# A fused conditional block on one core: the first sum of the ff activations as a ScalarE copy and an accumulating DMA

## The chip, the cores and the metric

The kernel runs on one core of a Trainium2 chip. The metric is the time of one execution on the device, in microseconds (us). The engines are TensorE (PE in the profile; its weight loads are PEld), VectorE (DVE), ScalarE (ACT), GpSimd (POOL) and SyncE (SP). Each works through its own queue in order; semaphores hold an instruction until what it needs is there, and everything behind it on that engine waits too.

## The reference

Two sequences of 2048 tokens with 512 features each pass one block. The modulation comes from a conditioning vector; then follow two residual branches, each with a normalization, two matrix products and a GELU:

```python
emb = jnp.dot(jax.nn.silu(t), ada_w) + ada_b
shift_msa, scale_msa, gate_msa, shift_mlp, scale_mlp, gate_mlp = jnp.split(emb, 6, axis=-1)
norm = _ln(x) * (1.0 + scale_msa[:, None]) + shift_msa[:, None]
h = jax.nn.gelu(jnp.dot(norm, ssm_w1) + ssm_b1, approximate=False)
x = x + gate_msa[:, None] * (jnp.dot(h, ssm_w2) + ssm_b2)
norm2 = _ln(x) * (1.0 + scale_mlp[:, None]) + shift_mlp[:, None]
hf = jax.nn.gelu(jnp.dot(norm2, ff_w1) + ff_b1, approximate=True)     # 512 -> 1024
x = x + gate_mlp[:, None] * (jnp.dot(hf, ff_w2) + ff_b2)              # 1024 -> 512
```

All is float32.

## The kernel before, in words

**Blocks and stages.** The 4096 tokens are cut into eight blocks of 512. Each block has four products: `hA` (x times `ssm_w1`), `oA` (its result times `ssm_w2`, added to x), `hC` (times `ff_w1`) and `oC` (times `ff_w2`, added to x). The gates are multiplied into the second weights beforehand. The stages of neighbouring blocks are interleaved: in step i of the loop over blocks (it starts at 1) come the products `hC` of block i, `oA` of block i+1, `oC` of block i, and `hA` of block i+2.

**Products of quarters.** Instead of eight products of quarter matrices a stage makes seven (named P1 to P7), whose operands are sums and differences of quarters. Where a quarter's product is cut once more in the same way, its seven smaller products are called leaves. For the activations of `hC` (the tile `hClo`, `hChi`: features on partitions, tokens in columns) the operands of the first level are made by `sums_of_first` (L388), once for each of two groups of features:

```python
lambda: cut_sum(eng, s[0], q["21"], q["22"], ALU.add, cut),        # P5
lambda: cut_sum(eng, s[1], s[0], q["11"], ALU.subtract, cut),      # P6
lambda: cut_sum(eng, q["21"], q["11"], q["21"], ALU.subtract, cut),# P7, in place
lambda: cut_sum(eng, s[2], q["12"], s[1], ALU.subtract, cut),      # P3
```

Each is one addition or subtraction of 128 partitions by 512 columns (L386). `q["21"]` is the second half of the group's columns in `hClo`, two runs of 256 floats on each partition; `q["22"]` the same in `hChi`; the three sums `s` lie in a tile `hSC` of their own. `first_operands` (L406) names them: P5 is `s[0]`, P4 is `q["22"]`, P7 is `q["21"]`.

**The order of the work.** Nothing is reordered by a scheduler: the program's order is the order in each engine's queue. Work for the other engines is hung into TensorE's stream by `hook(hooks, places, ops)` (L583): after the matmuls of a place (a number in the products of `hC`, a step name such as P1 or R4 in `oA`, a mark such as 0a in `oC`) the ops listed there are issued. `residual_with_leaves` (L906) runs the steps of `oA` in the order P1, R0, P5, R1, R2, P6, R3, R4, P7, R5, R6, and maps a hook's name to its step by `STEP_OF` (P2 to step P5, P5 to R4, P3 to R5, P4 to R6).

**Around the change.** In blocks 2, 3 and 5 (`SEVEN`, L1602) the last product `oC` is made wholly of leaves (`residual_in_all_leaves`, L1117). Its left operands need three layers of sums, all made on POOL:
- the four first-level sums of group 0, hung at place 20 of the `hC` products (L1685), and those of group 1, hung into `oA` (L1690);
- `sums24`, `sums356` and `sums17`: the leaves' sums of P2 and P4, of P5, P6 and P3, and of P1 and P7. Their first two steps go into `oA` (L1696, L1697) and, for `sums17` (written to a tile `leaves`, in block 5 to a free weight tile), to place 0a of `oC` (L1764). There, ahead of `sums17`, POOL also makes the power that gives the reciprocal root of the next normalization (`r`, L656), from a variance `ve` that DVE makes (L655) when the last row of `oA` is done.

Beside this ScalarE applies the GELU to the activations (L1278), normalizes a later block (L719), fills the accumulators with the bias (L529) and, after the first leaves of `oA`, copies an accumulator (`pl_oA_x` from `pl_oA_y`, L950) that TensorE goes on adding to. SP moves the transposed pieces of a later block (L739, `x<-blocks`, sixteen DMAs of 64 KB) at the same time. POOL begins no DMA.

Of the kernel before, what the change touches and what calls it, by code (L numbers as in the profile page):

```python
# [38 lines left out]
ALU = mybir.AluOpType  # L39
# [101 lines left out]
def kernel(  # L141
# [16 lines left out]
    nc = tc.nc  # L158
# [229 lines left out]
    def sums_of_first(q, s, eng, cut=1):  # L388

        return [  # L390
            lambda: cut_sum(eng, s[0], q["21"], q["22"], ALU.add, cut),
            lambda: cut_sum(eng, s[1], s[0], q["11"], ALU.subtract, cut),
            lambda: cut_sum(eng, q["21"], q["11"], q["21"], ALU.subtract, cut),
            lambda: cut_sum(eng, s[2], q["12"], s[1], ALU.subtract, cut),
        ]
# [146 lines left out]
    def apart_leaves(row, eng):  # L542
        v = row.rearrange("p (q e d) -> p q e d", q=2, e=2)
        eng.tensor_tensor(leaf_row, v[:, :, 1], v[:, :, 0], ALU.subtract)
# [38 lines left out]
    def hook(hooks, places, ops):  # L583

        for n, op in enumerate(ops):
            hooks.setdefault(places[min(n, len(places) - 1)], []).append(op)
# [623 lines left out]
    class First:  # L1210
# [29 lines left out]
        def __call__(self, p, j, k):  # L1240
            return self.ops[p][:, k, j * P : (j + 1) * P]

    class Second:
# [66 lines left out]
        def summed(self, g, eng, cut=1):  # L1310
# [4 lines left out]
            self.parts[g] = first_operands(q, s)  # L1315
            return sums_of_first(q, s, eng, cut)

        def __call__(self, p, j, k):
            return self.parts[k // 2][p][:, k % 2, j * P : (j + 1) * P]

# [138 lines left out]
    hooks = {}  # L1459
# [21 lines left out]
    hooks = {}  # L1481
# [28 lines left out]
    hooks = {}  # L1510
# [18 lines left out]
    hooks = {}  # L1529
# [12 lines left out]
    hC = Second(0)  # L1542
    n2[1] = Norm(1, 2)
    hooks = {}
# [25 lines left out]
    hooks = {}  # L1570
# [10 lines left out]
    hooks = {}  # L1581
# [7 lines left out]
    hooks = {}  # L1589
# [28 lines left out]
    for i in range(1, NBLK):  # L1618
        five, seven = True, i in SEVEN
        nxt, nx2, last = i + 1 < NBLK, i + 2 < NBLK, i + 1 == NBLK  # L1620
        ahead, alone = i + 3 == NBLK, not nx2
        hC = Second(i)
        hooks = {}
# [58 lines left out]
            hook(hooks, (4,), [lambda: apart_leaves(gb[5], nc.gpsimd)])  # L1682
        if i == 1:
            hook(hooks, (4,), [lambda: apart_leaves(gb[5], nc.gpsimd)])
        hook(hooks, (20,), hC.summed(0, nc.gpsimd))  # L1685
        hC.products(fa, fb[i], hooks, last or i == 1)

        hooks = {}
        hC_sums = hC.summed(1, nc.vector if alone else nc.gpsimd)
        hook(hooks, EARLY, hC_sums)  # L1690
        engs = (nc.vector if alone else nc.gpsimd, nc.gpsimd, nc.gpsimd)
        if seven:
# [12 lines left out]
        if nx2:  # L1705
# [26 lines left out]
            if ahead:  # L1732
                hooks = {}
# [10 lines left out]
        hooks = {}  # L1744
# [107 lines left out]
        hooks = {}  # L1852
# [81 lines left out]
```

## Time and profile before

| | before |
|---|---|
| median of 3 runs | 577.88 us (577.78 to 578.2) |
| the profiled execution | 577.74 us, its span 575.9 us |
| mean granted TensorE clock | 1.000 |
| DMA moved in the span | 62.30 MB, 108 GB/s on average |
| DMA queues | SP's and ScalarE's |

The profile is that of one execution, its span being the time from the first to the last instruction; the measured time of the same execution holds 1.8 us more. A row of the timeline gives the start, the duration, the engine, the line of the kernel, the operation, the tile written and the tiles read, the shape and the count; in square brackets the idle time ahead of it and what ended that. Rows that follow one another without a gap are merged and counted (x16). A row of groups gives the count, the busy time in us and the mean in ns, and then the idle time ahead and its releasers. Tile names are shortened: `hSC` is a tile of first-level sums, `forms` a buffer that holds the leaves' sums, `fw` and `w` are weights. An engine with `q` behind its name (SPq, ACTq) is the issuing of a DMA, not its transfer.

### The profile page before, as it was taken

The numbers are of one execution on the slowest core, as the hardware profiler recorded it, in microseconds if no ns is written. First come the engines' busy times: TensorE is split into PE (matmuls) and PEld (weight loads), VectorE is DVE, ScalarE is ACT, GpSimd is POOL, SyncE is SP. The second block draws the span as 40 slices with busy tenths as digits, with TensorE's granted clock in tenths as the row PEclk, the third lists the DMA queues.
The fourth block names the chain that finished last, engine by engine and source line by source line (L and its number), as shares of the span: only waits on it lengthen the run. The fifth ranks groups of instructions, "written<-read, shape, count | busy, mean of one in ns | idle before, by whom it ended". The sixth has DMA issues, their size and how long they took to land.

```text
span 575.9 us, 10119 instructions
## 1 busy us (share of the span) xinstructions
PE 570.8 (99%) x3443; PEld 514.1 (89%) x3443; DVE 453.6 (79%) x963; ACT 292.7 (51%) x574; POOL 436.7 (76%) x460
## 2 busy tenths in 40 slices
PE   8999999999999999999999999999999999999997
PEld 4888888888899889998899988998889999899897
DVE  4968898996878586987869877996768598897676
ACT  3727457705652875448734588326655431742430
POOL 1665449999949869889898999998994885379361
PEclk9999999999999999999999999999999999999999
DMA  8977333303205223283032930243240240031002
GB/s 329 390 232 249 100 71 92 96 38 146 58 18 162 106 100 69 97 260 126 1 93 50 330 115 21 54 109 122 101 109 2 110 126 23 1 73 74 2 1 73
DMA packets 26863, 62.30 MB, mean 108 GB/s; under 512 B 5136, under 2 KB 6204, under 8 KB 25148
## 3 DMA queue, kind: packets, MB, share of 16 engines
q1 hardware_dynamic: 22784, 55.87, 29.9%
q10 hardware_dynamic: 4028, 5.79, 3.9%
q8 instruction: 27, 0.44, 0.4%
q14 instruction: 24, 0.20, 0.1%
HBM read 35.94 MB, written 9.97 MB: 80 GB/s over the span
## 4 chain that ended last, share of the span: by engine, by line
PE 97%; DMA 2%; SPq 0%; DVE 0%; issue 0%; DVEq 0%
PE px_hC L1283 11%; PE py_hA L565 10%; PE py_hC L1283 8%; PE pv_hC L1283 8%; PE pl_oC_P_y L1038 5%; PE py_oC L990 5%; PE pv_hA L565 5%; PE py_oA L925 5%; PE pl_oC_A_y L1133 4%; PE py_oA L565 4%; PE pl_oC_P_v L1038 3%; PE pl_oC_B_y L1133 3%; PE py_hC L565 2%; PE px_hA L565 2%; PE py_oC L565 2%; PE pl_oA_y L940 2%
## 5 line engine op out<-in xcount | busy, mean ns | idle before, releaser
L656 POOL TENSOR_TENSOR r<-ve,minus_half 128x4 f32<-128x4 f32 x16 | 16.6, 1037 | 57.7 <-DVE ve L655 50.7
L767 ACT ACTIVATE nT<-nT,mod,mod 128x512 f32<-128x512 f32 x32 | 23.4, 803 | 46.2 <-DMA nT<-blocks 16.3
L1206 POOL TENSOR_TENSOR forms<-forms 128x256 f32<-128x256 f32 x56 | 42.5, 759 | 3.8 <-DVE forms L1202 0.4
L1283 PE MATMUL py_hC<-forms,fw 128*128 128x256 f32 x168 | 40.9, 379 | 0.0
L1300 DVE TENSOR_TENSOR hClo<-hClo,py_hC 128x512 f32<-128x512 f32 x42 | 28.5, 683 | 11.6 <-ACT hClo L1297 8.2
L719 ACT ACTIVATE nT<-x,nmr,rstd 128x512 f32<-128x512 f32 x36 | 26.8, 803 | 19.4 <-DVE nmr L704 16.8
L1283 PEld LDWEIGHTS py_hC<-forms,fw 128*128 128x128 f32 x168 | 31.7, 190 | 4.6 <-DVE hClo L1300 0.2
L386 POOL TENSOR_TENSOR hSC<-hClo,hChi 128x512 f32<-128x512 f32 (+1 forms) x16 | 19.2, 1205 | 18.7 <-ACT hChi L1278 17.9
L602 DVE BATCH_NORM_STATS2 st<-x 128x6 f32<-128x512 f32 x42 | 28.4, 675 | 4.9 <-DMA x<-in_x_dram 4.9
L1300 DVE TENSOR_TENSOR hChi<-hChi,pv_hC 128x512 f32<-128x512 f32 x35 | 23.2, 678 | 9.2 <-PE pv_hC L1283 5.0
L1278 ACT ACTIVATE hClo<-hClo,colsT 128x256 f32<-128x256 f32 x56 | 25.3, 498 | 5.0 <-DVE hClo L1300 4.8
L1283 PE MATMUL px_hC<-forms,fw 128*128 128x256 f32 x112 | 27.6, 379 | 0.0
L767 ACT ACTIVATE x<-x,mod 128x512 f32<-128x512 f32 x24 | 17.5, 801 | 18.8 <-DMA x<-blocks 18.8
L386 POOL TENSOR_TENSOR hClo<-hClo 128x512 f32<-128x512 f32 (+1 forms) x23 | 26.5, 1154 | 0.0
L1278 ACT ACTIVATE hChi<-hChi,colsT 128x256 f32<-128x256 f32 x56 | 25.1, 496 | 1.9 <-DVE hChi L1300 1.9
L730 DVE STREAM_TRANSPOSE blocks<-nT 128x512 f32<-128x512 f32 x36 | 24.2, 695 | 1.7 <-ACT nT L719 1.7
L1297 ACT ACTIVATE hChi<-py_hC 128x512 f32<-128x512 f32 x14 | 7.6, 594 | 34.0 <-PE py_hC L1283 14.8
L1297 ACT ACTIVATE hClo<-px_hC 128x512 f32<-128x512 f32 x21 | 12.5, 596 | 22.5 <-PE px_hC L1283 18.9
L1283 PEld LDWEIGHTS px_hC<-forms,fw 128*128 128x128 f32 x112 | 21.3, 190 | 2.9
L565 PE MATMUL py_hA<-x,w 128*128 128x256 f32 x96 | 22.7, 379 | 0.0
L1300 DVE TENSOR_TENSOR hChi<-hChi,px_hC 128x512 f32<-128x512 f32 x28 | 19.1, 682 | 4.3 <-ACT hClo L1297 2.1
L1283 PE MATMUL px_hC<-forms,fw_s 128*128 128x256 f32 x84 | 20.5, 380 | 0.0
(537 smaller groups left out, 1921.9 us busy)
## 6 DMA issues: line engine op xcount, KB each, us to landing
x<-in_x_dram SPq DMA_DIRECT2D x13, 1024.0 KB
out_dram<-x SPq DMA_DIRECT2D x14, 512.0 KB
x<-blocks SPq DMA_DIRECT2D x96, 64.0 KB
nT<-blocks SPq DMA_DIRECT2D x88, 64.0 KB
ada<-in_L_cond_ada_w_dram SPq DMA_DIRECT2D x5, 1024.0 KB
fw<-in_L_cond_ff_w_dram SPq DMA_DIRECT2D x2, 2048.0 KB
nT<-blocks ACTq DMA_DIRECT2D x56, 64.0 KB
w<-in_L_cond_ssm_w_dram SPq DMA_DIRECT2D x2, 1024.0 KB
```

Source lines behind the costliest of these rows:

```text
L386: eng.tensor_tensor(out[:, r], a[:, r], b[:, r], f)
L565: nc.tensor.matmul(ps[b][j * apart][:, j, :], lhs(p, j, k), rhs(p, j, k), start=(fresh and j * (not apart) == 0 and k == 0), stop=(p in (" ...
L602: nc.vector.bn_stats(st, xs[self.i][:, c, :])
L767: nc.scalar.activation(dst, src, AF.Identity, bias=shift, scale=scale)
L925: nc.tensor.matmul(ps[BANK[p]][:, j, :], hops(p, j, k), wops[p][:, k, :], start=False, stop=(k == KD // 2 - 1), skip_group_check=True,)
L990: yield lambda j=j, k=k: nc.tensor.matmul(ps[BANK[p]][:, j, :], hops(p, j, k), wops[p][:, k, :], start=False, stop=(k == kdim - 1), skip_g ...
L1038: nc.tensor.matmul(t[:, n, :], hops.leaves[p][f][:, k, :], leaf_wops[p][f][:, k, :], start=room not in started, stop=(f in ("P2", "P3", "P ...
L1133: nc.tensor.matmul(rooms[g, b][:, at[p], :], hops.leaves[p][f][:, k, :], leaf_wops[p][f][:, k, :], start=(g, b) not in started, stop=(f in ...
L1206: eng.tensor_tensor(reg[d], reg[a], reg[b], ALU.add if f == "+" else ALU.subtract)
L1278: nc.scalar.activation(h, h, AF.Gelu_apprx_tanh, bias=fb1T[:, m : m + 1])
L1283: nc.tensor.matmul(ps[b][:, j, :], fa[ra][:, j * P : (j + 1) * P], fb[rb].rearrange("p a (c q) -> p c a q", q=Q), start=(fresh and j == 0) ...
L1300: nc.vector.tensor_tensor(dest(d), dest(d), ps[b], op)
```

## The change

In blocks 2, 3 and 5 the first sum of each group (P5 = P7 + P4) is no longer an addition on POOL. ScalarE copies one operand into the sum's place, and then a DMA that POOL begins adds the other operand to it. The other three sums of each group stay on POOL, but the order changes: the third sum, which overwrites P7 and needs only the copy to be done, comes directly after the DMA's issue; the second and fourth sums of both groups, which need the DMA's result, go to later hooks of `oA`.

```diff
+        def added_by_dma(self, g):
+
+            p = self.parts[g]
+
+            def op():
+                nc.scalar.copy(p["P5"], p["P7"])
+                nc.gpsimd.dma_start(out=p["P5"], in_=p["P4"], accum_op=ALU.add)
+
+            return op
...
-        hook(hooks, (20,), hC.summed(0, nc.gpsimd))
+        sums_0 = hC.summed(0, nc.gpsimd)
+        if seven:
+            sums_1 = hC.summed(1, nc.gpsimd)
+            adds = [hC.added_by_dma(g) for g in range(2)]
+            hook(hooks, (20,), [adds[0], sums_0[2]])
+        else:
+            hook(hooks, (20,), sums_0)
         hC.products(fa, fb[i], hooks, last or i == 1)
 
         hooks = {}
-        hC_sums = hC.summed(1, nc.vector if alone else nc.gpsimd)
+        if seven:
+            hC_sums = [adds[1], sums_1[2], sums_0[1], sums_0[3], sums_1[1], sums_1[3]]
+        else:
+            hC_sums = hC.summed(1, nc.vector if alone else nc.gpsimd)
         hook(hooks, EARLY, hC_sums)
```

`EARLY` is P1, P2, P6, P5, P7, so the six ops of `hC_sums` go to the steps P1, P5, P6, R4, P7 and P7 of `oA`. On ScalarE the copy of group 0 comes behind the first bias copy into `py_oA` (L529), the copy of group 1 behind the last GELU of the block and ahead of the copy of `pl_oA_x` (L950). One such DMA takes 128 rows of two runs of 1 KB, 256 KB.

## The prediction

> **What bounds the kernel now.** I read the page's first lines and its chain that ended last, then the waits of TensorE, then busy time by stretches around blocks 2, 3 and 5.
>
> ```profile
> PE 570.8 (99%) x3443; PEld 514.1 (89%) x3443; DVE 453.6 (79%) x963; ACT 292.7 (51%) x574; POOL 436.7 (76%) x460
> ...
> PE 97%; DMA 2%; SPq 0%; DVE 0%; issue 0%; DVEq 0%
> ```
> ```profile
> engine line waited for: us in total, times, longest us
> PE idle L1392 <- POOL w_t masks.py:199: 1.3, 1, 1.3
> PE pada L304 <- DMA ada<-in_L_cond_ada_w_dram: 0.3, 1, 0.3
> ```
> ```profile
> core 0: us, PE busy (x) PEld busy (x) DVE busy (x) ACT busy (x) POOL busy (x), PEclk, DMA share, GB/s
> ...
> 215.00:262.00 47.00, 47.00 (x335) 44.55 (x334) 37.95 (x101) 24.68 (x48) 41.92 (x40) 1.00 0.46 135
> 283.00:330.00 47.00, 47.00 (x335) 44.55 (x334) 38.93 (x101) 23.55 (x45) 43.12 (x41) 1.00 0.45 138
> 422.00:480.00 58.00, 58.00 (x400) 54.64 (x399) 42.74 (x110) 24.41 (x46) 44.37 (x44) 1.00 0.29 90
> ```
>
> TensorE makes 97% of the chain. Its whole list of waits is 1.6 us, both before the first block. In the three stretches that the edit touches it is busy for 47.00 of 47.00, 47.00 of 47.00 and 58.00 of 58.00 us at a granted clock of 1.00. The edit leaves TensorE's stream as it is. So it can win nothing there; all it can do is make TensorE wait. The question is which operand comes late, and by how much.
>
> **The change part by part.** It removes two of POOL's additions a block (six in all), adds two ScalarE copies and two DMAs that POOL begins, and moves what is left: the new POOL order is DMA of group 0, third sum of group 0, DMA of group 1, third sum of group 1, second and fourth of group 0, two `sums24`, second and fourth of group 1, two `sums356`, then as before the power `r` (L656) and two sums into `leaves`. Block 2 on POOL, and TensorE's reader of `leaves` (its weight load):
>
> ```profile
> 217.83 1.27 POOL L386 TENSOR_TENSOR hSC<-hClo,hChi 128x512 f32<-128x512 f32 x1
> ...
> 230.49 1.82 POOL L386 TENSOR_TENSOR forms<-hSC,hSC 128x768 f32<-128x768 f32 x1
> 232.39 1.81 POOL L386 TENSOR_TENSOR forms<-forms,hSC 128x768 f32<-128x768 f32 x1
> 236.48 1.02 POOL L656 TENSOR_TENSOR r<-ve,minus_half 128x4 f32<-128x4 f32 x1 [2.28 <-DVE ve L655]
> ...
> 238.82 1.27 POOL L386 TENSOR_TENSOR leaves<-leaves,hClo 128x512 f32<-128x512 f32 x1
> ```
> ```profile
> 240.22 0.53 PEld L1133 LDWEIGHTS pl_oC_B_y<-w_s,leaves 128*128 128x128 f32 x4
> ```
>
> Ten additions fill 217.83 to 230.49, 1.266 us each; two of 768 columns end at 234.20, 3.71 after 230.49. POOL then stands for 2.28 us until DVE's `ve`, so 2.28 us of lateness cost nothing. After that nothing is spare: `r` at 236.48 leads to `leaves` done at 238.82 + 1.27 = 240.09, 3.61 later, and TensorE loads it at 240.22, 0.13 after.
>
> *The copies.* ScalarE around the place:
>
> ```profile
> 217.91 0.58 ACT L529 COPY py_oA<-gb 128x512 f32<-128x512 f32 x1
> 218.42 0.81 ACT L719 ACTIVATE x<-x,nmr,rstd 128x512 f32<-128x512 f32 x1
> ...
> 222.05 0.89 ACT L1278 ACTIVATE hChi<-hChi,colsT 128x256 f32<-128x256 f32 x2
> 222.85 0.47 ACT L950 COPY pl_oA_x<-pl_oA_y 128x384 f32<-128x384 f32 x1
> ```
> ```profile
> L719 ACT ACTIVATE x<-x,nmr,rstd 128x512 f32<-128x512 f32 x24 | 18.9, 803 | 1.4 <-POOL nmr L671 1.4
> ...
> L849 ACT ACTIVATE hA<-hA 128x512 f32<-128x512 f32 x7 | 4.4, 626 | 2.9 <-DVE hA L848 2.9
> ```
> ```profile
> 425.40 0.91 ACT L1278 ACTIVATE hClo<-hClo,colsT 128x256 f32<-128x256 f32 x2 [0.34 <-DVE hClo L1300]
> ```
> ```profile
> 426.39 1.27 POOL L386 TENSOR_TENSOR hSC<-hClo,hChi 128x512 f32<-128x512 f32 x1 [0.87 <-ACT hClo L1278]
> ```
>
> No row shows an SBUF-to-SBUF copy of 128x512. The nearest is L849, the same shape in place, 0.63 us; L719, which also reads a scale and a bias, takes 0.80. ScalarE's instructions overlap by 0.09 (222.05 + 0.89 against 222.85), so a copy holds its queue for 0.54 (0.71 at the upper end). I take 0.54. ScalarE shows no idle entry from 217.91 to 222.85, so every copy moves all behind it. The first copy goes in at 218.42. The second stands ahead of the copy of `pl_oA_x` and behind the last gelu: it starts at 222.85 + 0.54 = 223.39 and ends at 224.02. POOL sees a ScalarE result 0.08 us after its end (425.40 + 0.91 = 426.31 against 426.39), here at 224.10. The copy of `pl_oA_x` ends at 223.93 + 0.47 = 224.40, seen at 224.48, and TensorE wants it at 224.38:
>
> ```profile
> 224.38 0.38 PE L940 MATMUL pl_oA_x<-w,hA 128*128 128x128 f32 x2
> ```
>
> That is 0.10 us of waiting, and it lies inside the larger delay below.
>
> *The wait put on POOL.* POOL's queue is in order, so all sums now stand behind the second copy, up to 224.10; the first DMA and the third sum of group 0 fill only a part of the time before. Let D be what issuing one DMA holds POOL for. The first D is hidden in that wait. After 224.10 come D, seven additions (8.86) and the two of 768 columns (3.71): `r` may start at 236.67 + D, where it started at 236.48. `leaves` is then done at 240.28 + D, seen at 240.36 + D, against 240.22. **TensorE loses D + 0.14 us in block 2.** The saved additions do not help, since the wait for the second copy is longer than they are. What follows shifts with TensorE, so the loss is neither repaid nor repeated.
>
> Block 3 has the same rows 68.0 us later:
>
> ```profile
> 290.87 0.47 ACT L950 COPY pl_oA_x<-pl_oA_y 128x384 f32<-128x384 f32 x1
> ```
> ```profile
> 304.49 1.02 POOL L656 TENSOR_TENSOR r<-ve,minus_half 128x4 f32<-128x4 f32 x1 [2.27 <-DVE ve L655]
> ```
> ```profile
> 308.24 0.53 PEld L1133 LDWEIGHTS pl_oC_B_y<-w_s,leaves 128*128 128x128 f32 x4
> ```
>
> The second copy ends 1.17 after the old start of L950 (0.54 + 0.63) as in block 2, so I take the same D + 0.14. In block 5 the loss is zero:
>
> ```profile
> 448.42 1.02 POOL L656 TENSOR_TENSOR r<-ve,minus_half 128x4 f32<-128x4 f32 x1 [10.36 <-DVE ve L655]
> ```
> ```profile
> 427.99 0.46 ACT L950 COPY pl_oA_x<-pl_oA_y 128x384 f32<-128x384 f32 x1 [0.82 <-PE pl_oA_y L940]
> ```
>
> There POOL stands for 10.36 us ahead of `r`, and ScalarE for 0.82 ahead of L950, room for the copy.
>
> *The size of D.* No DMA of the kernel before is begun by POOL, and none accumulates. Issues on the other two queues:
>
> ```profile
> 264.29 0.33 SPq L1615 DMA_DIRECT2D w_s<-park_pair  x1
> ```
> ```profile
> 220.00 10.01 SPq L739 DMA_DIRECT2D x<-blocks  x16
> ```
> ```profile
> 249.06 1.81 ACTq L1615 DMA_DIRECT2D w_s<-park_w  x1
> ```
>
> They hold their queue for 0.33, 0.63 (10.01 / 16) and 1.81 us. The lower end is 0, if POOL's cores go on meanwhile; below that there is nothing, as TensorE has no idle time to give back. The upper end is 1.81. I take 1.27, POOL's own time for one instruction over these 128x512 elements: it is the only row that shows what this engine spends on that much data, and it lies between the two larger issues.
>
> The Trainium skill ("DMA: Bandwidth & Descriptors", sections "SWDGE vs HWDGE vs iDMA" and "Latency and other measured facts") says that DMAs begun by GpSimd have their descriptors worked out by code on its cores, and that the first byte comes after about 1 us, against about 0.6 on the other path. No run here shows it; a D of 1.0 read off it would make the sum below 2.28 and the time 580.2, an estimate.
>
> **Sum:** 2 x (1.27 + 0.14) = 2.82 us. The profiled execution took 577.74 us (span 575.9 and 1.8 around it), so it would take 580.56; the median of the runs is 0.14 higher, so **580.7 us**, 0.5% slower.
>
> **The rivals.**
>
> *The issue is cheap (not slower).* If POOL's cores take up the next sum while descriptors are made elsewhere, D falls towards 0 and each block loses 0.14: 577.88 + 0.28 = 578.2. It decides at 0.2%, which is 1.16 us and about what a measurement of this kernel can tell from no change: 2D + 0.28 < 1.16, or D < 0.44. For it speaks the SP row with 0.33; against it that this row is of another engine, and that this transfer has 256 pieces (128 rows of two runs) and two operands.
>
> *The sum lands late.* The second sum of group 0 starts at 225.37 + D, 6.2 us after its DMA was issued (first copy seen at 219.13); that of group 1 five additions, 6.3 us, after. Where the landing takes longer, each us more is lost in blocks 2 and 3. Rows for its length:
>
> ```profile
> 420.91 10.01 SPq L739 DMA_DIRECT2D x<-blocks  x16
> ```
> ```profile
> 432.54 0.81 ACT L767 ACTIVATE x<-x,mod 128x512 f32<-128x512 f32 x1 [4.09 <-DMA x<-blocks]
> ```
> ```profile
> DMA packets 756, 1.06 MB, mean 88 GB/s; under 512 B 244, under 2 KB 244, under 8 KB 755
> ...
> q1 hardware_dynamic: 755, 1.05, 38.5%
> ```
>
> The last of sixteen 64 KB moves is issued near 430.29 and its reader starts at 432.54: 2.25 us. The DMA view of 219 to 231 us has 88 GB/s at a share of 38.5%, so 228 GB/s at full share: 64 KB are 0.29 us and the fixed part is 2.0. 256 KB are 1.15 alone, so 3.1 us in all, well hidden; with two operands and half the run length up to four times that, on the 61.5% that the block moves leave, 7.5, so 9.5. Against 6.2 + D that is up to 2.0 late, 4.0 in two blocks: up to 584.7.
>
> *The copy is dear.* At 0.71 instead of 0.54, twice a block, the second copy ends 0.34 later: 0.68 more in all, 581.4. This widens the forecast and is no case of its own.
>
> *The DMA does not shorten anything, but something else does (faster).* TensorE's list of waits has nothing to remove.
>
> **How the numbers follow.** Forecast (D from 0.44 to 1.81, copies at either price; 579.0 to 582.5): 0.60. Late landing (582 to 586): 0.19. Cheap issue (577.9 to 579.0): 0.18. Faster: 0.03. So slower by over 0.2%: 0.79; within: 0.18; faster: 0.03. The range takes the bounds of D and of the copy and most of the late landing: 578.3 to 584.7.
>
> **What would show it.** In the profile after: TensorE with a wait for POOL at `pl_oC_B_y<-...leaves` in blocks 2 and 3 of 1 to 2 us each, and none in block 5; POOL idle for 2 to 4 us ahead of the second DMA, waiting for ScalarE's copy; no idle of 2.28 us ahead of `r` in blocks 2 and 3; copies of 0.6 to 0.8 us; the first POOL addition after each DMA late by D. I would be wrong if POOL's addition follows the DMA at once, if POOL waits for the DMA itself, or if TensorE's wait is at another tile, `pl_oA_x` above all.

## The result, and the profile after

The changed kernel takes 581.91 us (median of 4 runs, 581.48 to 582.12) against 578.04 in the runs beside it (577.78 to 578.59): a ratio of 1.0065, 95% interval 1.0047 to 1.0082. It is slower, by 3.9 us; 580.7 was forecast, within 578.3 to 584.7.

The page of the changed kernel, its first lines, the new DMA queue and the chain:

```profile
PE 572.2 (99%) x3443; PEld 514.5 (89%) x3443; DVE 453.9 (78%) x963; ACT 295.7 (51%) x580; POOL 437.5 (75%) x460
...
q0 software_dynamic: 1632, 1.57, 1.9%
...
PE 86%; POOL 6%; ACT 4%; DMA 2%; DVE 1%; issue 0%; SPq 0%; DVEq 0%; POOLq 0%
```

POOL's busy time has not fallen: six additions went, and six DMA issues, which the profile books as POOL's work, came (460 instructions before and after). POOL and ScalarE now have 10% of a chain that was TensorE's before. The list of TensorE's waits has one new line, and that of its weight loads (PEld) a second, smaller place:

```profile
engine line waited for: us in total, times, longest us
PE pl_oC_B_y L1133 <- POOL leaves L386: 2.6, 2, 1.3
```
```profile
PEld pl_oA_x L940 <- ACT pl_oA_x L950: 0.5, 2, 0.3
```

The waits for POOL are two, in blocks 2 and 3, at the tile that the prediction named. The weight loads at which they stand:

```profile
242.13 0.52 PEld L1133 LDWEIGHTS pl_oC_B_y<-w_s,leaves 128*128 128x128 f32 x4 [1.51 <-POOL leaves L386]
```
```profile
311.86 0.52 PEld L1133 LDWEIGHTS pl_oC_B_y<-w_s,leaves 128*128 128x128 f32 x4 [1.51 <-POOL leaves L386]
```

They come 1.91 and 3.62 us later than before (240.22 and 308.24). Matched matmul by matmul, the two profiled executions are already 0.2 us apart ahead of block 2, a difference of their first microseconds. So block 2 loses 1.7 us (1.71) and block 3 another 1.7. Of each, 0.13 come already at `pl_oA_x`, where the prediction had 0.10 inside the larger delay, and the rest at `leaves`. The list's 1.3 is less than that rest because it counts from the booked end of the matmul ahead; without a wait the rows overlap, at this place by 0.17 before the change. POOL in block 2 shows where the delay comes from:

```profile
219.54 1.41 POOL L1324 DMA_DIRECT2D hSC<-hChi  x1 [1.47 <-ACT hSC L1323]
220.55 1.72 POOL L386 TENSOR_TENSOR hClo<-hClo 128x512 f32<-128x512 f32 x1
224.47 1.20 POOL L1324 DMA_DIRECT2D hSC<-hChi  x1 [2.20 <-ACT hSC L1323]
225.24 1.73 POOL L386 TENSOR_TENSOR hClo<-hClo 128x512 f32<-128x512 f32 x1
226.47 1.72 POOL L386 TENSOR_TENSOR hSC<-hSC,hClo 128x512 f32<-128x512 f32 x1
228.27 1.27 POOL L386 TENSOR_TENSOR hSC<-hChi,hSC 128x512 f32<-128x512 f32 x1
...
238.45 1.04 POOL L656 TENSOR_TENSOR r<-ve,minus_half 128x4 f32<-128x4 f32 x1
```
```profile
223.56 0.60 ACT L1323 COPY hSC<-hClo 128x512 f32<-128x512 f32 x1
224.07 0.46 ACT L950 COPY pl_oA_x<-pl_oA_y 128x384 f32<-128x384 f32 x1
```

POOL stands for 1.47 and 2.20 us in front of the two issues, each time for ScalarE's copy; the 2.28 us of idle time ahead of `r` are gone. The rows after an issue need care: an addition is booked from before the issue's end and lasts 1.72, so an issue's hold is read from starts. From 224.47 to 228.27 are 3.80 us for one issue and two additions of 1.266: the issue holds POOL for 1.27 (e2 below has an addition in its place, and 3.81 us).

In block 5 there is a smaller loss that was not forecast:

```profile
445.75 1.89 PE L565 MATMUL px_hA<-x,w 128*128 128x256 f32 x8
447.77 0.45 PE L565 MATMUL py_hA<-x,w 128*128 128x256 f32 x1
```

The matmuls of one step end 1.73 after their start when the next step is ready (eight at 0.216); here the next step starts after 2.02, 0.3 us late. From its second matmul on, matched with the kernel before, TensorE has lost 0.37. SP's rows and the reader of its moves:

```profile
424.53 11.56 SPq L739 DMA_DIRECT2D x<-blocks  x16
```
```profile
437.69 0.82 ACT L767 ACTIVATE x<-x,mod 128x512 f32<-128x512 f32 x1 [5.65 <-DMA x<-blocks]
```

Issuing the sixteen block moves takes 11.56 us instead of 10.01, and ScalarE waits 5.65 for them instead of 4.09. DVE makes the sums of the next `hA`'s operands behind ScalarE, in the changed kernel and before:

```profile
439.24 1.81 DVE L386 TENSOR_TENSOR nS<-x 128x512 f32<-128x512 f32 x1 [0.57 <-ACT x L767]
...
446.96 0.66 DVE L386 TENSOR_TENSOR x<-x 128x512 f32<-128x512 f32 x1
```
```profile
442.79 0.66 DVE L386 TENSOR_TENSOR x<-x 128x512 f32<-128x512 f32 x1
```

With the 3.63 us that everything here is later by, the last of them (`x<-x`, the third sum, made in place) starts 0.54 us late. It ends at 447.62, and the late step begins at 447.77.

### The profile page after: what moved, and what is told of

The parts are those of the page before. It is cut to its first block, busy times and chain, and to the rows that moved or that the text cites. A ratio compares the mean times of both kernels' runs of the same rounds, so it can differ in the third digit from the quotient of the medians.

```text
span 580.3 us, 10138 instructions
## 1 busy us (share of the span) xinstructions
PE 572.2 (99%) x3443; PEld 514.5 (89%) x3443; DVE 453.9 (78%) x963; ACT 295.7 (51%) x580; POOL 437.5 (75%) x460
## 4 chain that ended last, share of the span: by engine, by line
PE 86%; POOL 6%; ACT 4%; DMA 2%; DVE 1%; issue 0%; SPq 0%; DVEq 0%; POOLq 0%
PE py_hA L565 10%; PE px_hC L1283 10%; PE py_hC L1283 7%; PE pv_hC L1283 7%; PE pl_oC_P_y L1038 5%; PE py_oC L990 5%; PE pv_hA L565 5%; PE py_oA L565 4%; PE pl_oC_P_v L1038 3%; PE py_oA L925 3%; PE pl_oC_A_y L1133 2%; PE py_hC L565 2%; PE px_hA L565 2%; PE py_oC L565 2%; PE pl_oC_B_y L1133 2%; POOL forms L386 2%
## 5 line engine op out<-in xcount | busy, mean ns | idle before, releaser
L1300 DVE TENSOR_TENSOR hClo<-hClo,py_hC 128x512 f32<-128x512 f32 x42 | 28.5, 683 | 11.6 <-ACT hClo L1297 8.2
L386 POOL TENSOR_TENSOR hClo<-hClo 128x512 f32<-128x512 f32 (+1 forms) x23 | 29.2, 1274 | 0.0
L386 POOL TENSOR_TENSOR hSC<-hClo,hChi 128x512 f32<-128x512 f32 (+1 forms) x10 | 11.6, 1165 | 17.9 <-ACT hChi L1278 17.9
L386 POOL TENSOR_TENSOR hSC<-hSC,hClo 128x512 f32<-128x512 f32 (+1 forms) x16 | 20.2, 1268 | 0.7 <-POOL hSC L386 0.3
```

The costliest lines, as they stand in the source:

```text
L386: eng.tensor_tensor(out[:, r], a[:, r], b[:, r], f)
L1300: nc.vector.tensor_tensor(dest(d), dest(d), ps[b], op)
```

## The experiments

The theory: TensorE waits for `leaves`, the last of POOL's sums; they are late because POOL's in-order queue stands behind ScalarE's second copy and then is held by the DMA's issue. The rivals: the order alone; the landing or traffic of the DMA; the copies' weight on ScalarE.

**e1_order_alone.** The new order, but the first sum as a POOL addition.

```diff
-                nc.scalar.copy(p["P5"], p["P7"])
-                nc.gpsimd.dma_start(out=p["P5"], in_=p["P4"], accum_op=ALU.add)
+                nc.gpsimd.tensor_tensor(p["P5"], p["P7"], p["P4"], ALU.add)
```

> The new order of the sums in blocks 2, 3 and 5, with the first sum of each group as a POOL addition again: no copy and no DMA. Theory (the loss comes from POOL's queue standing behind ScalarE's second copy and from the DMA's issue): POOL's power r is reached at 236.1 in the times of the kernel before, ahead of DVE's variance (r started at 236.48), so TensorE has no wait at leaves and the time is 577.9 to 578.4 us. Rival (the order itself, the late second and fourth sums, is what TensorE waits for): the wait at leaves of 1.3 us in blocks 2 and 3 stays, about 580.6 to 581.5 us.

577.77 us (11 runs; before 577.77; ratio 0.9999, 0.999 to 1.0007), and TensorE has no wait at `leaves`. The order costs nothing.

**e2_copy_then_pool_add.** The copies stay, the DMA becomes a POOL addition in the same place.

```diff
-                nc.gpsimd.dma_start(out=p["P5"], in_=p["P4"], accum_op=ALU.add)
+                nc.gpsimd.tensor_tensor(p["P5"], p["P5"], p["P4"], ALU.add)
```

> As the changed kernel, but the second operand is added by a POOL addition of 128x512 in the place of the DMA: the copies and the wait for them stay, the issue and the landing go. Theory: the wait for the second copy stays and an addition of 1.27 us stands where the DMA's issue held POOL for 1.27 (1.50 with the 0.23 by which it starts later), so blocks 2 and 3 still lose 1.2 to 1.5 us each, with TensorE waiting for POOL at leaves; block 5 loses nothing, since no accumulating DMA slows the sixteen block moves there. Together 580.4 to 581.2 us. Rival (the DMA's landing or its traffic is the cost): 577.9 to 578.5 us.

581.04 us (ratio 1.006, 1.0047 to 1.0074): 3.3 of the 3.9 us are there without any DMA. That is inside the expected time; the loss, matched as above, is 1.6 us in each of blocks 2 and 3, a little above the 1.2 to 1.5. Its waits of TensorE, POOL in block 2, and SP in block 5:

```profile
PE pl_oC_B_y L1133 <- POOL leaves L386: 2.4, 2, 1.2
```
```profile
224.09 1.27 POOL L1324 TENSOR_TENSOR hSC<-hSC,hChi 128x512 f32<-128x512 f32 x1 [2.42 <-ACT hSC L1323]
...
238.22 1.02 POOL L656 TENSOR_TENSOR r<-ve,minus_half 128x4 f32<-128x4 f32 x1
```
```profile
424.18 10.03 SPq L739 DMA_DIRECT2D x<-blocks  x16
```

`r` comes 0.23 us earlier than with the DMA; 0.15 of that is the difference of the two executions ahead of block 2, so the addition in the issue's place wins 0.08, no more. The block moves take 10.03 again, and block 5 loses nothing. The landing is no cause in blocks 2 and 3.

**e3_group0_only.** The DMA for group 0 alone.

```diff
-            hC_sums = [adds[1], sums_1[2], sums_0[1], sums_0[3], sums_1[1], sums_1[3]]
+            hC_sums = [sums_1[0], sums_1[2], sums_0[1], sums_0[3], sums_1[1], sums_1[3]]
```

> Copy and DMA for group 0 alone; the first sum of group 1 is a POOL addition again, in the place where the second DMA was issued. Theory: POOL no longer stands behind the second copy; the issue for group 0 and its third sum end at about 221.9 (times of the kernel before), the sums of group 1 start at 222.2, r is reached at 236.1, so there is no wait at leaves in blocks 2 and 3, and one DMA in block 5 delays the block moves by half as much as two: 577.9 to 578.4 us. Rival (every DMA costs its issue on the path): half of the loss, about 580 us.

578.88 us (ratio 1.002, 1.0011 to 1.0029), half a microsecond above the expected range, and far less than half of the loss.

```profile
222.80 1.27 POOL L386 TENSOR_TENSOR hSC<-hClo,hChi 128x512 f32<-128x512 f32 x1 [0.67 <-ACT hClo L1278]
...
237.05 1.04 POOL L656 TENSOR_TENSOR r<-ve,minus_half 128x4 f32<-128x4 f32 x1
```

POOL waits here not for a copy but for the GELU behind the first copy: that copy moved ScalarE's queue by 0.5 us, the sums of group 1 begin at 222.80 instead of the 222.2 that I had reckoned with, and TensorE waits 0.2 us at `leaves` in each block, by the matched matmuls a loss of 0.45. The rest of `r`'s lateness is that the ten operations from 222.80 to 237.05 take 14.25 us, where 13.9 had been reckoned. In block 5 the moves take 10.66 us, about half of the stretch, and TensorE loses nothing there. The expectation had left out that a copy delays what stands behind it on its own engine.

**e4_block5_only.** The two conditions `if seven` of the change become `if i == 5`.

> The change in block 5 alone; blocks 2 and 3 as before. Theory: no wait at leaves; the two accumulating DMAs stretch the sixteen block moves from 10.0 to about 11.6 us, and TensorE waits some 0.3 to 0.4 us for the third sum of the next hA's operands (P7), once: 578.2 to 578.5 us. Rival (the 0.37 us in block 5 of the changed kernel was chance or came from the blocks ahead of it): 577.9 to 578.1 us. Rival (all three blocks lose alike): about 579.3 us.

578.61 us (ratio 1.0015, 1.0006 to 1.0024), 0.1 above the expected range. The loss of block 5 is there without the others:

```profile
421.02 11.79 SPq L739 DMA_DIRECT2D x<-blocks  x16
```
```profile
444.26 1.10 PE L565 MATMUL py_hA<-x,w 128*128 128x256 f32 x4
```

Against 443.85 before, the step is 0.41 late, and 0.49 from its second matmul on; 0.12 of that is there from the start of the execution, so block 5 loses 0.37. A further 0.4 us appears in the next block's `px_hC` products at 490 us, where TensorE waits for DVE; in the changed kernel it was 0.1. What sets it is left open.

**e5_second_in_two.** The DMA of group 1 is begun as two DMAs of half the data.

```diff
-                nc.gpsimd.dma_start(out=p["P5"], in_=p["P4"], accum_op=ALU.add)
+                if g:
+                    for k in range(2):
+                        nc.gpsimd.dma_start(out=p["P5"][:, k], in_=p["P4"][:, k], accum_op=ALU.add)
+                else:
+                    nc.gpsimd.dma_start(out=p["P5"], in_=p["P4"], accum_op=ALU.add)
```

> As the changed kernel, with the second DMA of each block begun as two DMAs of half the data each (128 pieces of 1 KB instead of 256). The data moved and the wait for the copy stay; one more issue stands in POOL's queue behind the second copy. Theory (POOL's hold for an issue is on the path, one for one): if the hold is mostly a fixed amount per DMA, 0.8 to 1.3 us more in each of blocks 2 and 3, 583.4 to 584.4 us; if it goes by the pieces, no more than 0.2 us a block, 581.6 to 582.2 us. The waits of TensorE at leaves grow by as much as POOL is held longer. Rival (the issue is not on the path): 581.4 to 581.9 us, with POOL held longer and TensorE's waits unchanged.

585.55 us (584.65 to 586.34; ratio 1.0132, 1.0118 to 1.0145), above both expectations of the theory. POOL is held 0.6 us longer, between the fixed amount (0.8 to 1.3) and the amount by pieces (at most 0.2), as the start of `r` shows (238.81; ahead of block 2 this execution is 0.2 earlier than the changed kernel's):

```profile
224.25 1.78 POOL L1326 DMA_DIRECT2D hSC<-hChi  x2 [2.19 <-ACT hSC L1323]
...
238.81 1.04 POOL L656 TENSOR_TENSOR r<-ve,minus_half 128x4 f32<-128x4 f32 x1
```

TensorE's wait grew by the same 0.6 (1.89 against 1.32 at its matmul). That is 1.2 us in two blocks; the other 2.4 are of another kind. After the wait the matmuls ran at half speed:

```profile
239.99 0.61 PE L1133 MATMUL pl_oC_B_y<-fw_t,forms 128*128 128x128 f32 x4
242.49 0.71 PE L1133 MATMUL pl_oC_B_y<-w_s,leaves 128*128 128x128 f32 x4 [1.89 <-POOL leaves L386]
243.04 0.96 PE L1133 MATMUL pl_oC_B_y<-fw_t,leaves 128*128 128x128 f32 x4
243.79 1.06 PE L1133 MATMUL pl_oC_A_v<-w_s,forms 128*128 128x128 f32 x4
```
```profile
core 0: us, PE busy (x) PEld busy (x) DVE busy (x) ACT busy (x) POOL busy (x), PEclk, DMA share, GB/s
...
242.40:246.40 4.00, 3.91 (x21) 3.91 (x22) 4.00 (x11) 4.00 (x6) 4.00 (x4) 0.59 0.00 0
```

The mean granted clock over these 4 us is 0.59; at the same place in block 3 it is 0.57. Each drop costs 1.6 us by the shift of the later matmuls. Two of the four executions had a mean clock of 0.994 (586.28 and 586.34 us), two of 0.997 (584.65 and 584.83). One drop takes 0.41 of the clock for 4 us, which is 0.003 of the span, so this fits both drops in the first two and one in the others; only the first was profiled. That the length of the wait sets the drop off was not tried by itself.

**e6_plain_dma.** The DMAs overwrite instead of adding, so that P5 is P4 alone: the addition is left out.

```diff
-                nc.gpsimd.dma_start(out=p["P5"], in_=p["P4"], accum_op=ALU.add)
+                nc.gpsimd.dma_start(out=p["P5"], in_=p["P4"])
```

> The same copies and the same DMAs from POOL, but plain ones: they overwrite the copied operand instead of adding to it, so that P5 is P4 alone. Theory: POOL is held as long as by the accumulating DMA (1.2 us, within 0.2), so TensorE waits at leaves for 1.1 to 1.4 us in blocks 2 and 3 as in the changed kernel; the transfer lands earlier than after the 4.5 us of the accumulating one, which changes nothing on the path, and the block moves in block 5 are stretched less: 580.9 to 581.9 us. Rival (what accumulation adds to the issue is the cost): 579.5 us or less.

580.94 us (ratio 1.0056, 1.0042 to 1.007): at the lower end of the expected time, but not for the reason given. The lines of its DMAs, and SP in block 5:

```profile
L1324 POOL DMA_DIRECT2D hSC<-hChi x6: 722/743/951, 219.3 to 430.7; - x6
...
DMA to landing us min/median/max: 2.6/3.0/3.9
```
```profile
423.62 10.05 SPq L739 DMA_DIRECT2D x<-blocks  x16
```

The same two lines of the changed kernel:

```profile
L1324 POOL DMA_DIRECT2D hSC<-hChi x6: 1199/1222/1412, 219.5 to 431.6; - x6
...
DMA to landing us min/median/max: 4.2/4.5/4.8
```

A plain issue of the same pieces is booked for 0.74 us, 0.5 less than an accumulating one, and TensorE's wait is 1.0 instead of 1.3 a block. I had expected the same hold. The block moves are not stretched: with the same bytes moved, it is the accumulation that slows them.

**e7_power_later.** The first two sums into `leaves` go ahead of `r` on POOL.

```diff
-[lambda: n2[i + 1].root()] + sums17[:1] + (leaf_fold or [])[:-2])
+sums17[:2] + [lambda: n2[i + 1].root()] + (leaf_fold or [])[:-2])
...
-sums17[1:2] + [s[2] for s in (sums24, sums356, sums17)]
+[s[2] for s in (sums24, sums356, sums17)]
```

> As the changed kernel, but in blocks 2, 3 and 5 POOL makes the first two sums into leaves ahead of the power r instead of behind it. Theory (TensorE waits for leaves because they stand at the end of POOL's queue): leaves are ready 1.0 us earlier, so the wait there falls from 1.3 to about 0.3 us in blocks 2 and 3, 579.6 to 580.2 us, if the normalization behind r, now 2.6 us later, has that much room. Rival (it has not): the loss comes back at the sums that feed the next block's products, 580.5 to 583 us, with a wait of TensorE for forms or nT.

584.53 us (ratio 1.0113, 1.0098 to 1.0129), above the theory's range and the rival's too.

```profile
PE pl_oC_A_y L1133 <- DVE x L1151: 2.5, 2, 1.2
...
PE pl_oC_B_y L1133 <- DVE x L1151: 0.9, 2, 0.5
PE pl_oC_B_y L1133 <- POOL leaves L386: 0.6, 2, 0.3
```
```profile
242.09 0.17 DVE L700 TENSOR_TENSOR small<-r,small 128x4 f32<-128x4 f32 x1 [3.58 <-POOL r L656]
```

The wait at `leaves` falls from 1.3 to 0.3 a block, as the theory has it. But DVE's queue stands 3.58 us for `r`, with the additions behind it that empty the accumulators, and TensorE waits for those, 1.7 us a block. The rival was right that the room is missing, and wrong on the place: not the next block's operands but the accumulators of the running product.

**e8_copies_on_dve.** `nc.vector.tensor_copy` in the place of `nc.scalar.copy`.

> As the changed kernel, with the two copies on DVE instead of ScalarE. ScalarE's queue is as in the kernel before. Theory (the second copy's end starts the part of POOL's work that is on the path): DVE makes the second copy behind its first addition of oA, at about 222.8 in the times of the kernel before, ending at about 223.4 instead of 224.0; POOL's second issue and all behind it come 0.5 to 0.8 us earlier, and blocks 2 and 3 lose 0.9 to 1.3 us each instead of 1.69; the 0.11 us ahead of pl_oA_x go: 579.9 to 580.9 us. Rival (it is POOL's total work, not the wait for the copy): as the changed kernel, 581.5 us.

581.14 us (ratio 1.006, 1.0047 to 1.0072), 0.2 above the expected range.

```profile
222.91 0.42 DVE L1323 COPY hSC<-hClo 128x512 f32<-128x512 f32 x1
```
```profile
223.63 1.20 POOL L1324 DMA_DIRECT2D hSC<-hChi  x1 [2.75 <-DVE hSC L1323]
...
237.74 1.04 POOL L656 TENSOR_TENSOR r<-ve,minus_half 128x4 f32<-128x4 f32 x1
```

The second issue and `r` come 0.84 and 0.71 us earlier than in the changed kernel (0.77 and 0.64 without the 0.07 by which this execution is ahead before block 2). TensorE's wait at `leaves` is 0.8 a block instead of 1.3, and the matched loss 1.07 instead of 1.71, 0.64 less. So the wait for the copy is on the path, one for one from `r` on. Against that, the losses at the two places of e4 are there, 0.44 and 0.36 us.

Put side by side, block 2 of six kernels shows how the loss follows POOL. The start of `r` is without the difference of the executions ahead of block 2, the loss is that of the matched matmuls at `leaves`:

| | start of `r`, us | loss in block 2, us |
|---|---|---|
| changed kernel | 238.26 | 1.71 |
| e2 | 238.18 | 1.62 |
| e3 | 236.99 | 0.45 |
| e5 (without the clock's share) | 238.83 | 2.28 |
| e6 | 237.91 | 1.35 |
| e8 | 237.62 | 1.07 |

Each time the loss is the start of `r` less 236.55, within 0.01 us. In e1 and in the kernel before `r` starts at 236.48, and nothing is lost.

None of these beats the kernel before: TensorE has no wait there to remove.

## Why the prediction was right, point by point

- **What bounds the kernel: right.** TensorE's stream is unchanged and could only be made to wait. e1, with the same reordering and no copy or DMA, takes the time of before.
- **The place: right.** POOL waits for the second copy, reaches `r` late, and TensorE waits at `leaves` in blocks 2 and 3. e8 shows the wait for the copy as a cause, e2 that an addition in the issue's place loses nearly as much, e5 and e6 that the issue's length counts: each moves TensorE by what it moves `r`.
- **The issue's hold: right in size, by a choice and not by a row.** 1.27 was taken, as POOL's time for an addition over the same elements; 1.27 is measured. That they agree is luck: the plain issue over the same elements is booked for 0.74, so the time of an addition does not set the hold. The Trainium skill's 1 us to the first byte ("DMA: Bandwidth & Descriptors", "Latency and other measured facts") gave the lower estimate of 580.2; no row here shows a first byte, and the holds lie on both sides of that figure.
- **The loss per block: 1.41 forecast, 1.7 measured.** The mis-sized term is the start of `r`. POOL books the issue 0.31 us after the copy's end (223.56 + 0.60 = 224.16 to 224.47), where an addition follows a ScalarE result after 0.08: 0.23 more, which the prediction had at nothing. The seven operations from 228.27 to 238.45 take 10.18 us instead of 6.33 + 3.71 = 10.04: 0.14 more. The copy is a little cheaper: its successor starts after 0.51, not 0.54. Together 0.3, which is the difference. From `r` to the loss the prediction was right: the other kernels lose as the table says.
- **Block 5: the step "the loss is zero" failed.** `leaves` and `pl_oA_x` were right there. What it left out is that the accumulating DMAs run beside SP's block moves, whose reader in block 5 already waits for them before the change (4.09 us). The moves take 1.55 us longer, and TensorE loses 0.37. With a POOL addition (e2) or plain DMAs (e6) the moves take 10.03 and 10.05 and that loss is gone; alone in block 5 (e4) it stays. That the delay passes through ScalarE's modulation and DVE's sums is read from their rows and was not tried by itself; it is not one for one either, since in e5 the moves take only 10.82 and TensorE loses 0.35 there, with 1.29 instead of 0.66 us booked for DVE's `x<-x`.
- **The late landing: did not happen.** It took 4.5 us, 4.8 at most; the first reader in block 2 starts 6.9 us after the issue (219.54 to 226.47). The estimate of up to 9.5 was twice too high.
- **The cheap issue: did not happen.** POOL goes on only when the issue is done; even with the plain issue of 0.74 the kernel is slower by 0.56%.

Twice 1.71, 0.37 in block 5 and 0.08 in the products at 490 us make 3.87, the 3.9 us between the medians. The forecast had 2.82: the rest is twice 0.3 from the start of `r` and 0.45 from block 5 on.

## What to carry to other kernels

To replace an operation by a hand-over to two other engines, count the wait for the first of them, not the work saved: here an addition of 1.27 us was exchanged for an issue of 1.27 us, and nearly all of the loss is the in-order queue standing for the copy, with the sums behind it. A gap on a helper engine (2.28 us ahead of `r`) is all that such a wait may use; what has to fit in it is the delay of the last sum in the queue. And before an instruction is moved ahead on one engine, look at what the others do while they wait for the one that it passes.

## What the runs showed of the hardware

- After a wait of 1.89 us (e5) TensorE's granted clock was 0.59 on average over 4 us and 0.50 from 243.2 to 246.5, which cost 1.6 us more than the wait; after the changed kernel's waits of 1.3 us it stayed at 1.00. By the mean clocks of e5's executions, two had such a drop at both places and two at one only. The Trainium skill ("TensorE: Matmul & The Clock Gate", Part 1) puts the fall to half clock after an idle window of about 3.4 us that runs freely; half the clock agrees, and so does the difference between executions, as far as the mean clocks show it; but here a shorter wait came ahead of the fall.
- A DMA begun by POOL that adds 256 KB to its destination is booked for 1.22 us on POOL (1.27 by the starts of what follows) and lands after 4.5; the same pieces copied are booked for 0.74 and land after 3.0. Two of half the size hold POOL 0.6 longer than one.
- Accumulating DMAs of 256 KB stretched the issue of another queue's sixteen moves in block 5 from 10.0 to 11.6 us (changed kernel) and 11.8 (e4), to 10.8 where the second was begun in halves (e5) and to 10.7 with one alone (e3); plain ones of the same size did not (10.05).
